# A four-layer graph network on one core: 28 destination blocks in seven full panels and 21 gathered, instead of 29 in eight panels and 20 gathered

## The chip, the core and the metric

The kernel runs on one core of a Trainium2 chip. The metric is the device time of one execution in microseconds (us). The engines are called as in the profile: PE is TensorE's matmul, PEld its weight load, DVE is VectorE, ACT is ScalarE, POOL is GpSimd and SP is SyncE. SP and POOL also issue the DMAs that matter here.

## What is computed

There are 6250 nodes with 256 features and 100,000 edges, sorted by destination. Each node's features are normalised and go through a relu. Then come four layers: each node adds up the features of its in-neighbours to its own, and a three-step MLP follows. The last layer's output is added to the input.

```python
def agg(h):
    return jax.ops.segment_sum(h[src], dst, num_segments=N)
for l in range(NL - 1):
    h = x + agg(x)
    h = jax.nn.relu(h @ W1s[l] + b1s[l])
    h = jax.nn.relu(h @ W2s[l] + b2s[l])
    x = h @ W3s[l] + b3s[l]
h = x + agg(x)
h = jax.nn.relu(h @ cW1 + cb1)
h = jax.nn.relu(h @ cW2 + cb2)
return h @ cW3 + cb3
...
h = jnp.maximum(_layernorm(x, axis=-1), 0.0)
x = x + _L0_gnn_ref(h, src, dst, ...)
```

## The kernel before

The 6250 nodes are cut into 49 blocks of 128 (the last has 106). The first matrix of a layer's MLP is applied before the sum over neighbours, since the two commute; W3 of one layer and W1 of the next are multiplied together once in the preparation. So a layer begins with a table of 49 blocks x 256 features, which lies in the chip's DRAM (`tables[l]`) and, split into a high and a low part, in SBUF (`XY`).

**Two ways to sum over neighbours.** For some destination blocks the edges are made into a dense matrix of counts, and the sum is a product with it: this is a *panel*. A panel is three or four destination blocks wide (384 or 512 columns). `product` runs over the 49 source blocks j; each j, called a *unit*, takes four matmuls (two halves of 128 features, high and low part) of the panel's width (L1334). The counts are bytes in DRAM (`mats`). `fetch` loads them in chunks of seven source blocks (L1033), and `prepare` turns each block into float on ACT or DVE (L1310, L1312) a few units ahead.

The other destination blocks are *gathered*. Each block's edges are held in 18 tiles of 128. For every tile POOL issues an indirect DMA that fetches the 128 source rows (L1198), and PE adds them up by products with a one-hot matrix that DVE makes (L1223, L1242: 44 small matmuls for a block). `finish` adds the block's own row, turns it over on PE, and after every four blocks calls `mlp`. All this is done by the class `Gathered`, one object for a layer.

**Which block goes where.** `gone` lists the gathered blocks as (first block, number), and `panels` the others. The last panel, blocks 44 to 47, is also the last but one entry of `gone`: in the first layer it is gathered, and afterwards it is a panel.

```python
gone = [(0, 4), (4, 4), (8, 4), (12, 4), (16, 3), (44, 4), (48, 1)]
panels = [(19, 3), (22, 4), (26, 4), (30, 4), (34, 3), (37, 3), (40, 4), (44, 4)]
```

The first layer thus has 7 panels (25 blocks) and 24 gathered blocks, the later ones 8 panels (29 blocks) and 20 gathered.

**The first layer builds the matrices.** The byte matrices are made beside the first layer, by `build`: 16 steps for each block of a panel, in each two matmuls of one-hots (L1010) and a copy of their result to bytes, three of four on ACT (L1017) and the fourth on DVE (L1019). `PRE` units of two steps each stand ahead of the first panel, as many as its matrices need and four more.

**The order of the work.** The whole instruction order is written out by hand. `now` counts units, `later(n, f)` puts work n units on, and `tick` runs what is due. `when` gives each unit a length in advance: the panel's width in blocks plus 2 (in the first layer a share for the building comes on top; a unit of `PRE` counts 7). A block's gathered work is cut into two *visits*, of 12 and of 6 tiles. A layer's first visit is put `LEAD` after its beginning in that measure, the last one `TAIL` units before the end of its last panel, and the others evenly between them by their number of tiles (`begin`, `advance`). POOL's gathers are issued two visits ahead in the first layer and three in the others (`ahead`, `send`), into 24 row buffers in the first layer and 26 in the others.

**The change of layer.** A gather reads rows from anywhere in the table, so the first gather of a layer has to wait until the last block of its table is stored. `mlp` puts the products of a group of blocks into fixed units, one group behind the other (`free`). When `store` has written the 49th block it calls the next layer's `begin`, and with it the first gathers are issued. PE in the meantime begins the next layer's first panel, with the source blocks that are already back in `XY` (`reload`, `bring`, `split`). The block 48, the last of `gone`, and the last panel are the last two groups of a layer.

Of the kernel before, what the change touches and what calls it, by code (L numbers as in the profile page):

```python
# [396 lines left out]
def sorted_edges(  # L397
# [65 lines left out]

    gone = [(0, 4), (4, 4), (8, 4), (12, 4), (16, 3), (44, 4), (48, 1)]
    panels = [(19, 3), (22, 4), (26, 4), (30, 4), (34, 3), (37, 3), (40, 4), (44, 4)]
    S0 = 2 * panels[0][0]
    assert gone[-2] == panels[-1] and sorted(
        b + i for b, n in gone[:-2] + gone[-1:] + panels for i in range(n)) == list(range(NT))  # L470
# [430 lines left out]
    with tc.manual_schedule():  # L901
# [57 lines left out]
        def pair(hots, k):  # L959

            if k < len(batches):
                s = batches[k][1]
                pairs[s] = hots.tile([P, 2, GSUB, 2], BF16, name="pairs", bufs=3)
                nc.scalar.copy(pairs[s], clT[:, :, :, s - S0, None].to_broadcast([P, 2, GSUB, 2]))
# [9 lines left out]
        def low_hot(hots, k):  # L974
            if k < len(batches):
                p, s, q0 = batches[k]
                lo = hots.tile([P, BATCH, P], BF16, name="lo", bufs=2)
                one_hot(lo, lanes, pairs[s][:, 1, q0:q0 + BATCH, :], P)
                hot[k] = [lo]

        def high_hot(hots, k):
            if k < len(batches):
                p, s, q0 = batches[k]
                hi = hots.tile([P, BATCH, HW], BF16, name="hi", bufs=2)
                one_hot(hi, cols, pairs[s][:, 0, q0:q0 + BATCH, :], HW)
                hot[k].append(hi)

        def build(hots, ats, ps_b):


            each = GSUB // BATCH
            pair(hots, 0)
            low_hot(hots, 0)
            high_hot(hots, 0)
            step = 0
            for k, (p, s, q0) in enumerate(batches):
                i, half = divmod(s - 2 * panels[p][0], 2)
                if half == 0 and q0 == 0:
                    at = ats.tile([P, NT, P], U8, name="at", bufs=2)
                lo, hi = hot.pop(k)  # L1000
                if q0 == 0:
                    pair(hots, k + each)
                for q in range(0, BATCH, 2):
                    if q == 0:
                        low_hot(hots, k + 1)
                    elif q == 2:
                        high_hot(hots, k + 1)
                    bp = ps_b.tile([P, W], F32, name="bp")
                    for m in range(2):
                        nc.tensor.matmul(bp[:, m * HW:(m + 1) * HW], lo[:, q + m, :],  # L1010
                                         hi[:, q + m, :], start=True, stop=True)
                    d = half * 64 + (q0 + q) * GD
                    o = at[:, :, d:d + 2 * GD].rearrange("p h (i d) -> p h i d", i=2)
                    v = bp[:, :2 * HW].rearrange("p (i h d) -> p h i d", i=2, d=GD)
                    step += 1
                    if step % 4:
                        nc.scalar.copy(o, v)  # L1017
                    else:
                        nc.vector.tensor_copy(o, v)  # L1019
                    if half and q0 + q + 2 == GSUB:  # L1020
                        own = at[:, panels[p][0] + i, :]
                        nc.vector.tensor_tensor(own, own, ident, OP.add)
                        nc.sync.dma_start(out=mats[p][:, i, :], in_=at.rearrange("p h d -> p (h d)"))
                    yield
# [133 lines left out]
        class Gathered:  # L1158
            def __init__(self, l):
                self.l, self.sent, self.done = l, 0, 0  # L1160
                self.first = None
                self.end = ends[l] - TAIL
                self.blocks = [(b, n, i, left[q] + i * T)
                               for q, (b, n) in enumerate(gone) for i in range(n)
                               if l == 0 or (b, n) != panels[-1]]
                self.own = {}
                self.visits = [(g, rounds) for g in range(len(self.blocks)) for rounds in VISITS[l > 0]]
                self.n = len(self.visits)
                self.rows = {}

                self.upto = [0]
                for _, rounds in self.visits:
                    self.upto.append(self.upto[-1] + 2 * len(self.tiles(rounds)))
# [3 lines left out]
                return sorted({k for r in rounds for k in ROUNDS[r] if k is not None})  # L1177

            def begin(self, t):
                self.first = when[t] + LEAD  # L1180
                self.pace = (when[self.end] - self.first) / (self.upto[-1] - self.upto[1])

            def send(self, upto):
# [95 lines left out]
        PRE = (GSUB * panels[0][1] + EARLY) // 2  # L1279
# [1 line left out]
        units = [(0, -1, j) for j in range(PRE)] + [  # L1281
            (l, p, j) for l in range(NLAYER + 1) for p in range(last[l] + 1) for j in range(NT)]
        ahead = [2, 3]
        LEAD, TAIL = 75, 8

        ends = [PRE + NT * sum(k + 1 for k in last[:l + 1]) for l in range(NLAYER + 1)]
        when = [0.0]
# [76 lines left out]
        with tc.tile_pool(name="hots", bufs=1) as hots, tc.tile_pool(  # L1364
            name="ats", bufs=1
        ) as ats, tc.tile_pool(name="rings", bufs=AHEAD + 2) as rings, tc.tile_pool(
            name="gath", bufs=24
        ) as gath, tc.tile_pool(
            name="ps_a", bufs=2, space=PSUM
        ) as ps_a, tc.tile_pool(name="ps_b", bufs=2, space=PSUM) as ps_b:  # L1370
            layers[0].begin(0)
            layers[0].send(ahead[0])
            beside = build(hots, ats, ps_b)
            while now[0] < PRE:
                for _ in range(2):
                    next(beside)
                    built[0] += 1
                tick()
                layers[0].advance()
                if built[0] == GSUB * panels[0][1]:  # L1380
                    for _ in range(3):
                        fetch(0, 0)
            for p in range(last[0] + 1):
                product(0, p, ps_a, beside)
            assert next(beside, None) is None and built[0] == total
# [13 lines left out]
def kernel(  # L1399
# [26 lines left out]
    good = keep.tile([1, 1], I32, name="good")  # L1426
    rest = (x, src, dst, W1s, b1s, W2s, b2s, W3s, b3s, cW1, cb1, cW2, cb2, cW3, cb3, out)
    sorted_edges(tc, good, *rest)
    done = nc.values_load(good[0:1, 0:1], min_val=0, max_val=1)
    with tc.If(done == 0):  # L1430
# [27 lines left out]
```

## Time and profile before

| | |
|---|---|
| median of 3 runs | 2232.75 us (2231.62 to 2237.27) |
| the profiled execution | 2230.63 us, its span 2228.8 us |
| granted TensorE clock, mean | 0.983 |
| panel matmuls L1334 | 6076 (3724 of 512 columns, 2352 of 384) |
| gathers L1198 | 1512, first at 144.7 us, last at 2200.4 us, median 953 ns |
| matmuls of gathered rows L1242 | 3696, 281.5 us busy |
| transposes L1264 | 168, 31.9 us busy |
| build matmuls L1010 | 928, 136.0 us busy |
| casts L1310 on ACT, L1312 on DVE | 943 and 576 |

The span is the time from the first to the last instruction of the profiled execution. The preparation lasts until about 145 us, the first layer until about 731 us, and the others end near 1230, 1727 and 2215 us. The time between two layers cannot be read from PE's busy share, since PE already works on the next layer's first panel while the last blocks of the old one are finished.

### The profile page before, as it was taken

The numbers are of one execution on the slowest core, as the hardware profiler recorded it, in microseconds if no ns is written. First come the engines' busy times: TensorE is split into PE (matmuls) and PEld (weight loads), VectorE is DVE, ScalarE is ACT, GpSimd is POOL, SyncE is SP. The second block draws the span as 40 slices with busy tenths as digits, with TensorE's granted clock in tenths as the row PEclk, the third lists the DMA queues.
The fourth block names the chain that finished last, engine by engine and source line by source line (L and its number), as shares of the span: only waits on it lengthen the run. The fifth ranks groups of instructions, "written<-read, shape, count | busy, mean of one in ns | idle before, by whom it ended". The sixth has DMA issues, their size and how long they took to land.

```text
span 2228.8 us, 35398 instructions
## 1 busy us (share of the span) xinstructions
PE 2118.0 (95%) x12356; PEld 1559.5 (70%) x12356; DVE 918.2 (41%) x2723; ACT 920.1 (41%) x1915; POOL 1521.5 (68%) x1570
## 2 busy tenths in 40 slices
PE   4778999999999999999999999999999999999998
PEld 2555766667776777778877777778877766677765
DVE  6667465445656522223323422223323423333332
ACT  3666565666667422223334322322324423222222
POOL 2337777777776477777774577777774577777773
PEclk9888999999999999999999999999999999999999
DMA  5436575565666655555655655555655655666663
GB/s 173 134 120 201 185 227 173 178 211 174 200 205 225 195 168 172 165 156 170 193 167 172 191 173 169 157 161 180 187 163 166 204 173 177 184 184 186 191 186 102
DMA packets 264100, 395.56 MB, mean 177 GB/s; under 512 B 36353, under 2 KB 210028, under 8 KB 263912
## 3 DMA queue, kind: packets, MB, share of 16 engines
q0 software_dynamic: 73920, 200.88, 30.2%
q1 hardware_dynamic: 187936, 189.68, 26.8%
q10 hardware_dynamic: 2056, 2.65, 0.4%
q8 instruction: 99, 1.62, 0.3%
q14 instruction: 89, 0.73, 0.1%
HBM read 335.81 MB, written 57.26 MB: 176 GB/s over the span
## 4 chain that ended last, share of the span: by engine, by line
PE 65%; DMA 4%; issue 2%; POOL 1%; ACT 0%; DVE 0%; SPq 0%; POOLq 0%; DVEq 0%
PE agg L1334 45%; PE sums L1242 8%; PE ps L1099 5%; PE ps L1122 4%; DMA rows<-table,idx 3%; POOL rows L1198 1%; PE ps L1119 1%; PE pt L1264 1%; PE bp L1010 1%; DMA xt<-in_x_dram 0%; ACT h L1347 0%; DMA own<-table 0%; DVE z L1127 0%; ACT at L1017 0%; ACT h L1268 0%
## 5 line engine op out<-in xcount | busy, mean ns | idle before, releaser
L1198 POOL DMA_INDIRECT rows<-table,idx x1512 | 1484.3, 982 | 614.0 <-issue 243.5
L1334 PE MATMUL agg<-a,XY 128*128 128x512 f32 (+1 forms) x6076 | 1454.7, 386 | 3.6 <-ACT a L1310 3.2
L1334 PEld LDWEIGHTS agg<-a,XY 128*128 128x128 f32 x6076 | 1085.4, 189 | 239.1 <-issue 81.0
L1310 ACT CAST a<-at 128x512 fp32r<-128x512 uint8 (+1 forms) x943 | 537.0, 579 | 650.3 <-PE agg L1334 585.2
L1312 DVE CAST a<-at 128x512 fp32r<-128x512 uint8 (+1 forms) x576 | 279.6, 490 | 498.7 <-PE agg L1334 455.0
L1242 PE MATMUL sums<-rows,hot 128*32 128x256 f32 x3696 | 281.5, 387 | 31.9 <-DMA rows<-table,idx 30.4
L1242 PEld LDWEIGHTS sums<-rows,hot 128*32 128x32 f32 x3696 | 119.4, 110 | 169.7 <-issue 54.7
L1017 ACT CAST at<-bp 128x392 uint8<-128x392 f32 x348 | 161.1, 490 | 142.8 <-PE bp L1010 139.9
L1099 PE MATMUL ps<-h,w 128*128 128x512 f32 (+5 forms) x392 | 164.3, 541 | 1.2 <-ACT h L1347 1.2
L1254 DVE TENSOR_TENSOR u<-sums,own 128x256 f32<-128x256 f32 x84 | 35.5, 423 | 291.7 <-PE sums L1242 291.7
L1010 PE MATMUL bp<-hi,lo 128*128 128x196 bf16 x928 | 136.0, 259 | 19.9 <-DVE hi L969 11.7
L1223 DVE TENSOR_TENSOR hot<-colf,rel 128x64 f32<-128x64 f32 x924 | 140.6, 217 | 12.3 <-PE sums L1242 11.9
L1122 PE MATMUL ps<-w,h 128*128 128x256 f32 x588 | 140.0, 379 | 0.0
L1010 PEld LDWEIGHTS <-lo 128*128 128x128 bf16 x928 | 71.9, 100 | 94.8 <-issue 43.9
L969 DVE TENSOR_TENSOR lo<-lanes,pairs 128x512 bf16<-128x512 bf16 x232 | 97.1, 419 | 84.0 <-PE bp L1010 58.4
L969 DVE TENSOR_TENSOR hi<-cols,pairs 128x784 bf16<-128x784 bf16 x232 | 129.6, 559 | 0.0
L1122 PEld LDWEIGHTS ps<-w,h 128*128 128x128 f32 x588 | 111.0, 189 | 15.7
L1268 ACT ACTIVATE h<-pt,bias 128x256 f32<-128x256 f32 (+1 forms) x92 | 36.9, 453 | 199.1 <-PE pt L1264 199.1
L1101 ACT ACTIVATE h<-ps,bias 128x512 f32<-128x512 f32 (+5 forms) x98 | 62.4, 637 | 109.6 <-PE ps L1099 109.6
L1131 DVE TENSOR_TENSOR zz<-ps,w 128x512 f32<-128x512 f32 (+1 forms) x81 | 51.7, 638 | 130.9 <-PE ps L1122 130.9
L1099 PEld LDWEIGHTS ps<-h,w 128*128 128x128 f32 (+1 forms) x392 | 68.2, 181 | 51.3 <-issue 29.4
L1019 DVE CAST at<-bp 128x392 uint8<-128x392 f32 x116 | 65.5, 565 | 91.9 <-PE bp L1010 90.3
(134 smaller groups left out, 716.6 us busy)
## 6 DMA issues: line engine op xcount, KB each, us to landing
at<-mat SPq DMA_DIRECT2D x133, 448.0 KB
at<-mat SPq DMA_DIRECT2D x84, 336.0 KB
rows<-table,idx POOLq DMA_INDIRECT x1512
mat<-at SPq DMA_DIRECT2D x29, 784.0 KB
table<-zz SPq DMA_DIRECT2D x66, 256.0 KB
back<-table SPq DMA_DIRECT2D x126, 128.0 KB
own<-table SPq DMA_DIRECT2D x80, 128.0 KB
xs<-in_x_dram SPq DMA_DIRECT2D x8, 768.0 KB
```

The costliest lines, as they stand in the source:

```text
L969: nc.vector.tensor_tensor(o.rearrange("p q (n t) -> p q n t", t=2), values.rearrange("p (n t) -> p n t", t=2)[:, None, :, :].to_broadcast( ...
L1010: nc.tensor.matmul(bp[:, m * HW:(m + 1) * HW], lo[:, q + m, :], hi[:, q + m, :], start=True, stop=True)
L1017: nc.scalar.copy(o, v)
L1019: nc.vector.tensor_copy(o, v)
L1099: nc.tensor.matmul(ps[:mp, :w], weights[l][0][:, c, i * P:i * P + mp], h1[:, c, :w], start=(c == 0), stop=(c == KC - 1))
L1122: nc.tensor.matmul(o, h2[0][:, c, nodes], w3[:, c, :], start=(c == 0), stop=(c == KC - 1))
L1198: nc.gpsimd.indirect_dma_start(out=t, out_offset=None, in_=tables[self.l][:, :], in_offset=bass.IndirectOffsetOnAxis(ap=idx[:, o:o + 1], a ...
L1223: nc.vector.tensor_tensor(hot[:, i, :, :], colf[:, None, i * Q:(i + 1) * Q].to_broadcast([P, 2, Q]), rel[:, o + k:o + k + TS + 1:TS, None] ...
L1242: nc.tensor.matmul(self.sums[(2 * h + m) * Q:(2 * h + m + 1) * Q, :C], self.hots[r, m][:, h, :], self.rows[g, h, k], start=(r == 0), stop= ...
L1310: nc.scalar.copy(o, mat[l, p][j])
L1312: nc.vector.tensor_copy(o, mat[l, p][j])
L1334: nc.tensor.matmul(agg[c][:, :w], XY[:, j, o:o + P], a[:, :w], start=(j == 0 and half == 0), stop=(j == NT - 1 and half == 1))
```

## The change

Block 19 goes from the panels to the gathered blocks. The remaining 28 blocks form seven panels of four, where there were eight panels of three or four. The first layer, which leaves the last panel out, has six panels (24 blocks) and 25 gathered blocks, the later ones seven panels and 21 gathered blocks.

```diff
-    gone = [(0, 4), (4, 4), (8, 4), (12, 4), (16, 3), (44, 4), (48, 1)]
-    panels = [(19, 3), (22, 4), (26, 4), (30, 4), (34, 3), (37, 3), (40, 4), (44, 4)]
+    gone = [(b, 4) for b in range(0, 20, 4)] + [(44, 4), (48, 1)]
+    panels = [(b, 4) for b in range(20, 48, 4)]
```

In the build, the copies of the steps ahead of the first panel all go to ACT. `PRE` grows from 28 units to 36 by itself, because the first panel now has four blocks.

```diff
                     step += 1
-                    if step % 4:
+                    if step % 4 or step <= 2 * PRE:
                         nc.scalar.copy(o, v)
```

The first and last visit of a layer are placed anew in the later layers; the first layer keeps 75 and 8.

```diff
-                self.end = ends[l] - TAIL
+                self.end = ends[l] - (TAIL if l else 8)
...
-                self.first = when[t] + LEAD
+                self.first = when[t] + (LEAD if self.l else 75)
...
-        LEAD, TAIL = 75, 8
+        LEAD, TAIL = 90, 2
```

## The prediction

> **What bounds the kernel now.** I read the page first. Its busy shares point at TensorE (PE), and the row of GpSimd (POOL) in the 40 slices has a shape worth following: 7 in nearly every slice, with a dip at each change of layer.
>
> ```profile
> PE 2118.0 (95%) x12356; PEld 1559.5 (70%) x12356; DVE 918.2 (41%) x2723; ACT 920.1 (41%) x1915; POOL 1521.5 (68%) x1570
> ...
> POOL 2337777777776477777774577777774577777773
> ```
>
> So I asked next what POOL's gathers (L1198) wait for. The columns are the total in us, the number of waits, and the longest of them.
>
> ```profile
> POOL rows L1198 <- issue: 243.5, 799, 0.3
> POOL rows L1198 <- DMA own<-table: 112.9, 3, 40.9
> POOL rows L1198 <- PE agg L1334: 90.8, 298, 0.3
> POOL rows L1198 <- PE sums L1242: 50.6, 166, 0.3
> POOL rows L1198 <- DVE lo L969: 41.5, 1, 41.5
> ```
>
> Of 1512 gathers only four wait longer than 0.3 us: the first one, and the first of each later layer. All others follow the one before after the same 0.3 us, whoever is named as the releaser; the name is then an accident. A queue that was held by a buffer or by PE would show waits of many lengths. The gathers stand back to back. The third view gives the busy time of L1198 alone, by stretch between those four waits.
>
> ```profile
> 144.00:713.00 569.00, 436.76 (x432) 0.97 0.62 198
> 713.00:746.00 33.00, 0.00 (x0) 1.00 0.40 120
> 746.00:1204.00 458.00, 347.89 (x360) 1.00 0.60 179
> 1204.00:1244.00 40.00, 0.00 (x0) 1.00 0.36 107
> 1244.00:1703.00 459.00, 349.09 (x360) 1.00 0.59 179
> 1703.00:1741.00 38.00, 0.00 (x0) 1.00 0.36 107
> 1741.00:2202.00 461.00, 350.60 (x360) 1.00 0.61 185
> ```
>
> The whole span is therefore 144.7 us before the first gather, four solid runs of gathers (1.317, 1.272, 1.275 and 1.281 us each), three gaps (33.4, 40.9 and 38.6), and 27 us behind the last gather. What happens in a gap is read from the timeline, here of the first.
>
> ```profile
> 711.89 0.95 POOL L1198 DMA_INDIRECT rows<-table,idx  x1 [0.30 <-issue]
> ...
> 719.11 1.50 PE L1242 MATMUL sums<-rows,hot 128*32 128x256 f32 x20
> ...
> 730.74 0.69 ACT L1347 ACTIVATE h<-agg,bias 128x512 f32<-128x512 f32 x1 [3.69 <-PE agg L1334]
> ...
> 746.21 0.95 POOL L1198 DMA_INDIRECT rows<-table,idx  x1 [33.38 <-DMA own<-table]
> ```
>
> The last visit's matmuls begin 6.3 us after the last gather has ended (14.1 and 11.6 in the two later gaps: PE is that far behind), and from there to the next layer's first gather it is 27.1, 26.8 and 27.0 us. PE is nearly full as well: it waits for rows only 31 times, 30.4 us in all. The two engines are close to balance, and POOL never pauses inside a layer.
>
> **What the change removes.** Per later layer, three panels of 384 columns and five of 512 become seven of 512; in the first, three and four become six. Either way that is 196 matmuls x (3 narrow - 2 wide). Their cadence is in the chain of waits:
>
> ```profile
> 1467.49 3.74 PE agg L1334 x16
> ...
> 1491.71 2.79 PE agg L1334 x16
> ```
>
> 0.234 us wide, 0.174 narrow, so 196 x (0.522 - 0.468) = 10.6 us a layer, 42 in all. The build loses 32 of 928 bp matmuls (136.0 us): 4.7. ACT and DVE lose 196 of 1519 casts, SP 28 of 217 chunk loads; none of the three is the path.
>
> **What it adds.** One more gathered block per layer: 18 gathers on POOL, 44 sums matmuls (281.5/84 = 3.4 us) and two transposes (31.9/84 = 0.4) on PE, and small work on DVE and ACT that their shares of 41% cover. For PE that is 3.7 us a layer, so PE wins 42 + 4.7 - 15 = 32 us net, and POOL gets 72 gathers more.
>
> The preparation treats 450 gather columns for 432; the list is ready at 111 us, and the first gather waits until 144.7 for the first table, so 34 us cover that.
>
> In the first layer 16 more build steps stand ahead of the first panel. 56 steps took 43 us (144.7 to 187.75); 72 at that rate take 55, fewer if the copies moved to ACT relieve DVE. Those 12 us are no cost while POOL, already gathering from 144.7, ends later than PE; without that cover (PE's last visit is at 719 now, POOL's run would end at 737) they would be paid whole. The wider leads and tails scale with the unit (4 matmuls of 0.234 for 4 of 0.174): 90/6 and 75/5 are both 15 units. They move when PE takes rows up, not when POOL asks for them.
>
> **Does POOL have room for them?** By the waits, no. Its next gather is always ready, so 18 more take 18 x 1.27 to 1.32 us, unless PE falls behind by the 24 to 26 row buffers, which it gets further from. Set against each other, PE's lateness of 14.1 us at the second gap would become 14.1 - 7 (PE's gain) + 5.6 (the visit put six units later) - 22.9 (POOL's addition) = -10 us: PE will wait for rows, and POOL's run sets the end. The 0.30 us behind every gather, also behind the first ones after a pause of 40 us, when nothing can be queued, says that it belongs to the gather.
>
> The Trainium skill speaks against this: "Trace Analysis", section "Identifying the Most-Contended Engine", takes occupancy as a fair measure of how near to its limit GpSimd is; by that rule the 76% of a layer (347.89 of 458) would leave a quarter of POOL free, and the time would be that of rival (1) below.
>
> **The gaps.** Check of the old one from the last visit on: sums 1.5, eight wide units 7.5, the one-block MLP 2.6, eight narrow units 5.6, the four-block MLP 7.6 (four groups of 1.88 and 1.89), last store to first gather 3.1 (1241.38 to 1244.45 in the second gap): 27.9 against 27. In the later layers the visit now stands two units before the end; the last panel's MLP queues behind block 48's, six units later. So 1.5 + 1.9 + 14 wide units 13.1 + 2.6 + 7.6 + 3.1 = 29.8, less the 0.9 that the check was over: 29. Landing of the last rows, not seen by itself, lies between 1.4 (in the last layer the matmuls begin 1.4 us after the last gather, unwaited) and 3.5 (PE's longest wait for rows); I take 2, nearer the row at the same place. Gap 31. The first layer keeps its tail of 8: 1.5 + 7.5 + 2.6 + 7.5 + 7.6 + 3.1 - 0.9 + 2 = 31 too. Three gaps: 93 for 112.9.
>
> **The end.** Now 27.2 us behind the last gather, 14.2 of them behind the last aggregation. Then: 2 + 1.6 + 1.9 + 14.2, and block 48's two small products ahead of the last panel's on PE (0.65, a relu 0.4 with its signal 0.35, 0.7): 21.8.
>
> **The sum.** 144.7 + 450 x 1.317 (592.7) + 31 + 378 x 1.272 (480.9) + 31 + 378 x 1.275 (482.0) + 31 + 378 x 1.281 (484.1) + 21.8 = 2299 us span, for 2228.8 now. The profiled run took 2230.63, 1.8 more than its span, and the median of the runs is 2.1 above that: **2302 us**, 3.1% slower.
>
> **Rivals.** (1) POOL has room after all, because the 0.3 us are hidden waits on PE; then PE's sum decides: 2232.75 - 32 = 2201. For it: PE at 95%, and 65% of the chain of waits on PE. Against it: no wait of any length between 0.3 and 33 us. (2) PE stays late at the ends of the layers, as it does now by 11 us on average, since waiting for single rows all through the layer costs it its gain; three gaps of 40 in place of 31: 2329. For it: the margin is only 10 us a layer; against it: PE's work shrinks and POOL's grows. (3) The gaps and the tail give all back: 72 gathers cost about 91 us, and gaps and tail hold 140 us in all, so two thirds of that would have to go, although each gap has 27 us of chained work; a time around 2233.
>
> **How the numbers follow.** Forecast 0.79, rival (1) 0.05, (2) 0.12, (3) 0.04. Less than 0.3% (7 us) cannot be told from no change here. Rival (1) gives faster 0.05, (3) no change 0.03 with the rest slower: slower 0.92. The low end: the cadence of the undisturbed gather, 0.953 + 0.30 = 1.257, in half of the excess (1584 gathers, mean 1.288: -25), and gaps 2 us shorter: 2270. The high end is rival (2): 2328.
>
> **What would show it.** 1584 gathers with no wait over 0.3 us but four; runs of about 593 and 481 to 484 us; gaps near 31; wide agg cadence still 0.234; PE's waits for rows up from 30 to some 100 us, spread over the layers. Runs of gathers shorter than 470 us, or waits of POOL inside a layer on PE sums, would prove me wrong.

## The result, and the profile after

The changed kernel takes 2311.69 us (median of 4 runs, 2306.47 to 2313.69) where the kernel before takes 2233.82: a ratio of 1.0344, 95% interval 1.0321 to 1.0366. The forecast was 2302. The profiled execution took 2306.47 us, its span 2304.5.

First the page of the changed kernel: busy time by engine, POOL's row of the 40 slices, and the rows of the panel matmuls and of the gathered ones.

```profile
PE 2138.5 (93%) x11696; PEld 1453.6 (63%) x11696; DVE 856.8 (37%) x2648; ACT 885.9 (38%) x1778; POOL 1598.4 (69%) x1642
...
POOL 2337777777776477777775577777775677777774
...
L1334 PE MATMUL agg<-a,XY 128*128 128x512 f32 x5292 | 1404.0, 411 | 2.7 <-ACT a L1310 2.2
...
L1242 PE MATMUL sums<-rows,hot 128*32 128x256 f32 x3872 | 345.5, 391 | 88.1 <-DMA rows<-table,idx 86.6
```

The row of the gathered matmuls in the kernel before:

```profile
L1242 PE MATMUL sums<-rows,hot 128*32 128x256 f32 x3696 | 281.5, 387 | 31.9 <-DMA rows<-table,idx 30.4
```

PE runs 660 instructions fewer and is still "busier", by 20 us. The gathered matmuls show how: four more blocks should have added 13 us, and they added 64. A visit's matmuls overlap when all rows are there; now they come one by one as rows land, and each counts alone. PE's busy time hides that it waits. Its waits for rows (us in total, times, longest) have gone from the first line to the second:

```profile
PE sums L1242 <- DMA rows<-table,idx: 30.4, 31, 3.5
PE sums L1242 <- DMA rows<-table,idx: 86.6, 96, 3.9
```

The gathers' waits on POOL (us in total, times, longest):

```profile
POOL rows L1198 <- issue: 263.6, 865, 0.3
POOL rows L1198 <- PE agg L1334: 109.5, 256, 30.9
POOL rows L1198 <- PE sums L1242: 67.7, 222, 0.3
POOL rows L1198 <- DMA own<-table: 62.7, 2, 32.1
POOL rows L1198 <- DVE lo L969: 41.3, 1, 41.3
```

The picture is that of before: the first gather, three changes of layer (one of them now put down to PE's agg), and 0.3 us everywhere else; a single wait of 1.2 us inside a layer is the exception. By stretch, L1198 alone:

```profile
144.00:740.00 596.00, 458.76 (x450) 0.96 0.61 191
740.00:772.00 32.00, 0.03 (x1) 1.00 0.41 128
772.00:1254.00 482.00, 366.52 (x378) 1.00 0.59 176
1254.00:1284.00 30.00, 0.00 (x0) 1.00 0.47 135
1284.00:1768.00 484.00, 367.63 (x378) 0.99 0.57 173
1768.00:1798.00 30.00, 0.00 (x0) 1.00 0.45 133
1798.00:2282.00 484.00, 368.27 (x378) 0.99 0.58 176
```

The gap after the second layer, in order of time:

```profile
1252.48 0.95 POOL L1198 DMA_INDIRECT rows<-table,idx  x1 [0.30 <-issue]
...
1256.87 1.50 PE L1242 MATMUL sums<-rows,hot 128*32 128x256 f32 x20
...
1261.71 0.70 ACT L1347 ACTIVATE h<-agg,bias 128x512 f32<-128x512 f32 x1
...
1284.34 1.16 POOL L1198 DMA_INDIRECT rows<-table,idx  x1 [30.90 <-PE agg L1334]
```

The same gap in the kernel before:

```profile
1202.48 1.03 POOL L1198 DMA_INDIRECT rows<-table,idx  x1 [0.30 <-issue]
...
1217.61 1.50 PE L1242 MATMUL sums<-rows,hot 128*32 128x256 f32 x20
...
1244.45 0.95 POOL L1198 DMA_INDIRECT rows<-table,idx  x1 [40.94 <-DMA own<-table]
```

The last visit follows the last gather's end (1253.4) by 3.4 us, where PE used to be 14.1 late, and the next gathers begin 27.5 us after it. So the account closes, from one profiled span to the other: the four runs of gathers 1943.9 to 2043.6 us, +99.7; the three gaps 112.9 to 93.6, -19.4; the end 27.3 to 23.1, -4.2; the start -0.4. Together +75.7, as much as the spans differ.

For the experiments it must be known that in the three groups of several kernels all runs were some 27% longer, the kernel before included (2836 to 2841 us), with waits of POOL for PE of up to 21 us inside the layers in the kept traces, so of these groups only ratios to the kernel before in the same group are given, and they are weak evidence.

### The profile page after: what moved, and what is told of

The parts are those of the page before. It is cut to its first block, busy times and chain, and to the rows that moved or that the text cites. A ratio compares the mean times of both kernels' runs of the same rounds, so it can differ in the third digit from the quotient of the medians.

```text
span 2304.5 us, 33758 instructions
## 1 busy us (share of the span) xinstructions
PE 2138.5 (93%) x11696; PEld 1453.6 (63%) x11696; DVE 856.8 (37%) x2648; ACT 885.9 (38%) x1778; POOL 1598.4 (69%) x1642
## 4 chain that ended last, share of the span: by engine, by line
PE 51%; DMA 11%; issue 4%; POOL 3%; DVE 0%; SPq 0%; ACT 0%; POOLq 0%; DVEq 0%
PE agg L1334 34%; DMA rows<-table,idx 11%; PE sums L1242 7%; PE ps L1099 5%; PE ps L1122 4%; POOL rows L1198 3%; PE ps L1119 1%; PE pt L1264 1%; PE bp L1010 0%; DMA xt<-in_x_dram 0%; DMA own<-table 0%; DVE xt L1112 0%; DVE z L1127 0%; SPq L506 0%; DVE h L1344 0%
## 5 line engine op out<-in xcount | busy, mean ns | idle before, releaser
L1198 POOL DMA_INDIRECT rows<-table,idx x1584 | 1561.2, 986 | 617.3 <-issue 263.6
L1334 PE MATMUL agg<-a,XY 128*128 128x512 f32 x5292 | 1404.0, 411 | 2.7 <-ACT a L1310 2.2
L1334 PEld LDWEIGHTS agg<-a,XY 128*128 128x128 f32 x5292 | 968.8, 190 | 294.3 <-issue 84.7
L1310 ACT CAST a<-at 128x512 fp32r<-128x512 uint8 x819 | 502.6, 622 | 711.4 <-PE agg L1334 650.1
L1242 PE MATMUL sums<-rows,hot 128*32 128x256 f32 x3872 | 345.5, 391 | 88.1 <-DMA rows<-table,idx 86.6
L1312 DVE CAST a<-at 128x512 fp32r<-128x512 uint8 x504 | 228.1, 458 | 534.6 <-PE agg L1334 488.3
L1242 PEld LDWEIGHTS sums<-rows,hot 128*32 128x32 f32 x3872 | 132.5, 110 | 283.4 <-DMA rows<-table,idx 162.1
L1099 PE MATMUL ps<-h,w 128*128 128x512 f32 (+2 forms) x364 | 163.1, 570 | 0.3 <-ACT h L1347 0.3
L1010 PEld LDWEIGHTS <-lo 128*128 128x128 bf16 x896 | 71.5, 100 | 96.5 <-issue 42.8
L1101 ACT ACTIVATE h<-ps,bias 128x512 f32<-128x512 f32 (+2 forms) x91 | 60.6, 667 | 114.2 <-PE ps L1099 114.2
L1019 DVE CAST at<-bp 128x392 uint8<-128x392 f32 x94 | 53.1, 565 | 100.3 <-PE bp L1010 99.3
```

The lines of the kernel that those rows point to most:

```text
L1099: nc.tensor.matmul(ps[:mp, :w], weights[l][0][:, c, i * P:i * P + mp], h1[:, c, :w], start=(c == 0), stop=(c == KC - 1))
L1101: later(2, lambda: nc.scalar.activation(h2[0][:mp, i, :w], ps[:mp, :w], AF.Relu, bias=b2[l][:mp, i:i + 1]))
L1198: nc.gpsimd.indirect_dma_start(out=t, out_offset=None, in_=tables[self.l][:, :], in_offset=bass.IndirectOffsetOnAxis(ap=idx[:, o:o + 1], a ...
L1242: nc.tensor.matmul(self.sums[(2 * h + m) * Q:(2 * h + m + 1) * Q, :C], self.hots[r, m][:, h, :], self.rows[g, h, k], start=(r == 0), stop= ...
L1310: nc.scalar.copy(o, mat[l, p][j])
L1312: nc.vector.tensor_copy(o, mat[l, p][j])
```

## Experiments

### The gathers alone

The kernel before, with 18 more gathers in each layer that nothing reads. In the first form they stand behind the first 18 visits, in the second behind every second visit. Panels, lead, tail and the build's copies stay as before.

```diff
+                    if self.sent % 2 == 0 and self.sent < 2 * T:
+                        t = spare.tile([P, C], F32, name="unread")
+                        o = self.blocks[g][3]
+                        nc.gpsimd.indirect_dma_start(
+                            out=t, out_offset=None, in_=tables[self.l][:, :],
+                            in_offset=bass.IndirectOffsetOnAxis(ap=idx[:, o:o + 1], axis=0),
+                        )
                     self.sent += 1
...
+        spare = ctx.enter_context(tc.tile_pool(name="spare", bufs=2))
...
-        gath = ctx.enter_context(tc.tile_pool(name="gath2", bufs=26))
+        gath = ctx.enter_context(tc.tile_pool(name="gath2", bufs=25))
```

(The first form has `if self.sent < T:`.)

> The kernel before, with 18 more gathers in each layer into a spare tile that nothing reads (one behind each of the first 18 visits) and one row buffer less; no work on PE, ACT or DVE is added. Theory: each run of gathers grows by 23 us, 92 in all, of which PE's lateness at the gaps (6, 14 and 12 us) hides up to 30: 2234 + 92 - 30 = 2296, between 2280 and 2325. Rival (POOL has room, the 0.3 us behind a gather is a hidden wait): no change, 2234 within 10.

Measured in the group: a ratio of 1.0411 (1.0370 to 1.0453). The forecast, divided by 2234, is 1.028 (1.021 to 1.041), so this stands at its upper edge.

> The same kernel as gathers_alone (before, with 18 unread gathers a layer more), run again for the same reason. Where the kernel before takes its 2234: theory 2296, between 2280 and 2325; rival (POOL has room) 2234 within 10.

Measured, again in a group: 1.0375 (1.0292 to 1.0459), inside the range.

> The kernel before with 18 more gathers in each layer that nothing reads, one behind every second visit, and one row buffer less; nothing on PE, ACT or DVE. Theory: runs of about 593, 482, 483 and 485 us as after the change, gaps of 29 to 33: 2305, between 2285 and 2322. Rival (POOL has room): 2234 within 10. If only PE's new order costs: 2234 as well.

Measured in a group: 1.0277 (1.0193 to 1.0361); the forecast as a ratio is 1.032 (1.023 to 1.039).

> The kernel of gathers_alone_even alone in its group, since all groups of several kernels ran 27% long and the one single kernel didn't. Theory (POOL's run sets the layer): four runs of gathers of about 593, 482, 483 and 485 us with no wait inside them, gaps of 29 to 33, waits of PE for rows up from 30 us; 2305, between 2285 and 2322. Rival (POOL has room, or only PE's new order costs): 2234 within 10, with waits of POOL inside the layers.

Measured, alone: 2306.38 us against 2234.86, a ratio of 1.0319 (1.0299 to 1.0339). The forecast was 2305. POOL's busy time by stretch (all its instructions), and of PE's waits the one for rows (us in total, times, longest):

```profile
144.00:741.00 597.00, 459.76 (x450) 0.96 0.61 193
741.00:772.00 31.00, 0.11 (x1) 1.00 0.38 116
772.00:1254.00 482.00, 366.41 (x378) 1.00 0.59 177
1254.00:1284.00 30.00, 0.51 (x2) 1.00 0.43 127
1284.00:1766.00 482.00, 365.97 (x378) 0.99 0.59 176
1766.00:1795.00 29.00, 0.00 (x0) 1.00 0.41 120
1795.00:2276.00 481.00, 365.52 (x378) 0.99 0.60 182
```

```profile
PE sums L1249 <- DMA rows<-table,idx: 67.0, 71, 2.6
```

PE's waits for rows have more than doubled, from 30.4 us, and its busy time is 2155.9 us for 2118.0 with the same 12356 matmuls. The runs of gathers and the gaps are those of the changed kernel within 3 us each, although nothing reads the added rows and PE, ACT and DVE are given exactly the work that they had before. One gather inside a layer waits 1.4 us, all others 0.3, so the missing row buffer does not show either. That settles the cause: 72 more entries in POOL's queue cost 71.5 us by themselves, and the rest of the change (32 us less work on PE, the lead, the tail, the copies) is worth nothing that shows: 1.0344 and 1.0319 have intervals that overlap. The 0.3 us behind each gather are no room.

An added gather also moves 128 KB, so the run itself tells the queue from PE's order, but not POOL's issuing from the transfer. The DMA packets in the traces do. In the three gaps of the kernel before, POOL starts the layer's second gather 1.25 us after the first, while the first packet of the first gather moves only 1.9 to 2.4 us after that gather's start: POOL keeps its cadence before any row has moved. And the transfers keep up. Counted by the bytes of the queue, the median time from POOL's end to a gather's last packet is 1.5 to 1.9 us in every quarter of every run of gathers (in this kernel, the kernel before and the changed one), and not longer at the end of a run than at its start. Transfers that were the limit would fall further and further behind.

### The gathers taken away

The changed kernel without the gathers of block 19; its matmuls read the block's own rows in their place.

```diff
                         for h in range(2):
+                            if self.blocks[g][0] == 16 and self.blocks[g][2] == 3:
+                                self.rows[g, h, k] = self.own[g][:, 0, :]
+                                continue
                             t = gath.tile([P, C], F32, name="rows")
```

> The changed kernel, but block 19's 18 gathers in each layer are left out; its matmuls read the block's own rows instead, so PE's work and order stay. Theory (POOL's back-to-back gathers set the time): 1512 gathers, runs of about 569, 458, 459 and 461 us as before the change, PE late again by some 8 us at each of the three gaps: 2312 - 92 + 25 = 2245, between 2215 and 2260. Rival (PE's order, the places of the first and last visits, or the panels' shape cost the time): nothing of that is changed, so 2300 or more.

Measured in the group: 1.0117 (1.0058 to 1.0176). The forecast as a ratio is 1.005 (0.991 to 1.012).

> The same kernel as no_gathers_19 (block 19's 18 gathers a layer left out, PE's work and order as after the change), run again because the runs of that group were 27% longer with the kernel before too, PE standing still for stretches of up to 20 us that no instruction in the trace ends. Where the kernel before takes its 2234: theory (POOL's back-to-back gathers) 2245, between 2215 and 2260; rival (PE's order or the shape of the panels) 2300 or more.

Measured, again in a group: 1.0071 (1.0032 to 1.0109).

> The kernel of no_gathers_19 once more, to have it where the kernel before takes its 2234 us. Theory (POOL's back-to-back gathers): 2245, between 2215 and 2260, with four runs of gathers of about 569, 458, 459 and 461 us. Rival (PE's order or the shape of the panels): 2300 or more, with shorter runs and longer gaps.

Measured, alone: 2280.86 us (2 runs) against 2236.94, a ratio of 1.0205 (1.0157 to 1.0254). This misses the forecast by 36 us, and lies outside its range. The runs of gathers did shrink, to 581, 460, 459 and 462 us, but the later gaps grew to 48.6 and 47.1 and the end to 42.7. The second gap of this kernel shows why:

```profile
1215.44 1.50 PE L1245 MATMUL sums<-own,hot 128*32 128x256 f32 x20
...
1217.43 1.14 POOL L1201 DMA_INDIRECT rows<-table,idx  x1 [0.31 <-issue]
...
1227.23 1.50 PE L1245 MATMUL sums<-rows,hot 128*32 128x256 f32 x24
...
1239.77 1.50 PE L1245 MATMUL sums<-rows,hot 128*32 128x256 f32 x20
```

POOL's last gather ends at 1218.6. PE by then has just finished block 19's second visit (`sums<-own`, with no rows to wait for) and has block 48's two visits still ahead, pinned to units 12 us apart: 21.2 us from the last gather to the last visit, where it was 3.4. I had taken block 19's gathers out where they stood, near the end of each layer. Up to there PE is held up by POOL as in the changed kernel, and its order is fixed, so it cannot do the rest sooner. The place of a gather in the layer matters as well as the number: time saved on POOL behind the point up to which PE was held is not saved. This is read off this one trace; no undisturbed run tests it. The steps of that expectation that failed: PE was put 8 us late at each gap, and came 21.2 and 19.5 us after the last gather in the two later ones (3.9 in the first); the end was taken as unchanged, and PE came 20.9 us late there too; and the first run shrank to 581 us, not 569, with a wait of 5.6 us on PE inside it. From one profiled execution to the other, the end makes up 20 us of the miss, the runs 12 and the gaps 9. The rival's 2300 was not reached either: some 31 of the 75 us came back with the gathers.

So I took the same number out evenly, one of the 18 tiles of 18 blocks in each layer:

```diff
+                            if h and k == 3 and g < T:
+                                self.rows[g, h, k] = self.own[g][:, 0, :]
+                                continue
```

> The changed kernel with as many gathers as before the change, the 72 left out spread evenly: the first 18 blocks of each layer gather 17 tiles, and the matmuls of the 18th read the block's own rows. PE's work and order stay. It differs from no_gathers_19 in that no hole stands at the end of a layer. Theory (POOL's run sets the layer): runs of 569, 459, 460 and 462 us, gaps of 31 to 40: 2228, between 2210 and 2250. Rival (the new order on PE costs the most, and 31 us are all that 72 gathers are worth, as no_gathers_19_c gave): 2280, not under 2265.

Measured in a group: 0.9739 (0.9661 to 0.9817), that is 2.6% faster than the kernel before there, where the forecast as a ratio is 0.997 (0.989 to 1.007). The rival, 1.014 or more, would have the new order on PE cost something, and this ratio shows no such cost. But it was seen only in a group: there, a kernel with one block more in the panels (below) has the same ratio of 0.9739, and alone that kernel gains nothing. What the even removal takes alone is open, so that taking the gathers away gives their time back is not shown.

### The split of the blocks alone

```diff
-                    if step % 4 or step <= 2 * PRE:
+                    if step % 4:
...
-                self.end = ends[l] - (TAIL if l else 8)
+                self.end = ends[l] - TAIL
...
-                self.first = when[t] + (LEAD if self.l else 75)
+                self.first = when[t] + LEAD
...
-        LEAD, TAIL = 90, 2
+        LEAD, TAIL = 75, 8
```

> The changed split of the blocks alone: lead 75 and tail 8 in all layers and the build's copies as before. Theory: the gathers are as many, so the four runs are the same; the gaps stay near 31 us, the end is some 5 us longer with the tail of 8: 2317, between 2305 and 2330. Rival (the later last visit, which puts the last panel's MLP behind block 48's, costs the time): 20 us or more below the changed kernel, 2290 or less.

Measured in the group: 1.0247 (1.0187 to 1.0308). The loss is there without the new lead, tail and copies. But the forecast as a ratio is 1.037 (1.032 to 1.043), so the ratio misses it, and meets the bound of the rival, 1.025 or less. The changed kernel itself was not in that group, so what these three are worth beside it is not measured. The single runs bound it: against the unread gathers, which keep the old lead, tail and copies, the changed kernel's three gaps are 2.9 us longer together, its end is 4.0 shorter and its runs are 2.5 longer. No 20 us lie in the later last visit there.

### One block the other way

The kernel before with 30 blocks in 8 panels and 19 gathered:

```diff
-    gone = [(0, 4), (4, 4), (8, 4), (12, 4), (16, 3), (44, 4), (48, 1)]
-    panels = [(19, 3), (22, 4), (26, 4), (30, 4), (34, 3), (37, 3), (40, 4), (44, 4)]
+    gone = [(0, 4), (4, 4), (8, 4), (12, 4), (16, 2), (44, 4), (48, 1)]
+    panels = [(18, 4), (22, 4), (26, 4), (30, 4), (34, 3), (37, 3), (40, 4), (44, 4)]
```

> The kernel before, moved the other way: block 18 goes from the gathered ones to the first panel, which becomes (18, 4); 30 blocks in 8 panels, 19 gathered. 72 gathers fewer; PE gets 196 x (0.234 - 0.174) - 3.7 = 8 us a layer more and 5 us of building. Theory: POOL is no longer the bound, PE's waits for rows (84 us with its weight loads) mostly go: 2234 + 37 - 50 = 2221, between 2195 and 2250, and POOL waits inside a layer for PE. Rival (PE's work alone sets the time): 2234 + 37 = 2271.

Measured in the group: 0.9721 (0.9691 to 0.9751). The forecast as a ratio is 0.994 (0.983 to 1.007), so this misses it.

> The kernel of one_more_in_panels (block 18 from the gathered ones to the first panel; 30 blocks in 8 panels, 19 gathered) where the kernel before takes its 2234. Theory: POOL with 72 gathers less is no longer the bound; PE has 37 us more work and loses most of its 84 us of waits for rows: 2221, between 2195 and 2250, with waits of POOL on PE inside the layers. Rival (PE's work alone counts): 2271.

Measured, again in a group: 0.9739 (0.9661 to 0.9817), a miss too.

> The kernel of one_more_in_panels alone in its group. Theory: four runs of gathers of at least 545, 435, 436 and 438 us, stretched by waits of POOL for PE, which is now the bound: PE's 37 us more work less most of its 84 us of waits for rows give 2221, between 2195 and 2250. Rival (PE's work alone counts, as its 95% say): 2271.

Measured, alone: 2236.77 us against 2235.75, a ratio of 1.0005 (0.9996 to 1.0014): no change, where the groups gave a gain of 2.6 to 2.8%. L1198 by stretch, and its two waits with times over 0.3 us inside the layers:

```profile
144.00:712.00 568.00, 426.68 (x414) 0.96 0.61 193
712.00:756.00 44.00, 0.18 (x2) 1.00 0.45 139
756.00:1207.00 451.00, 331.81 (x342) 1.00 0.58 174
1207.00:1256.00 49.00, 0.36 (x1) 1.00 0.42 123
1256.00:1711.00 455.00, 330.69 (x342) 0.99 0.57 172
1711.00:1760.00 49.00, 0.44 (x1) 1.00 0.42 123
1760.00:2197.00 437.00, 332.95 (x342) 1.00 0.63 189
```

```profile
POOL rows L1198 <- PE sums L1242: 92.3, 146, 6.0
...
POOL rows L1198 <- PE bp L1010: 29.5, 92, 1.8
```

This is what POOL looks like when it is not the bound: waits of up to 6 us on the matmuls that free its buffers, 1.32 us for a gather in the second run where 1.27 is POOL's own pace, and gaps of 44 to 49 us, in which PE comes 16 to 21 us late. Only the last layer, whose MLP is lighter, still runs at 1.278. From one profiled span to the other, PE's busy time grew by 21 us and its idle time shrank by 14. I had expected 37 more and 50 less; the sum missed by 16 us though inside its range. The 50 was taken from PE's waits and its weight loads' waits added together, but those overlap: PE's own were 30.4 us, of which 16.1 stayed.

So with 20 gathered blocks the kernel stands where POOL and PE meet. One block less changes nothing, one more costs 3.4%. No version that beats the kernel before was found.

## Why the prediction was right

**POOL bounds each layer.** The step that decided was the reading of the waits: no gather waits inside a layer, so each one added counts in full. The runs of gathers came out at 595.6, 481.5, 483.4 and 483.2 us for 592.7, 480.9, 482.0 and 484.1. The unread gathers reproduce it without any change on PE. Rival (1), that the 0.3 us are hidden waits, falls with them, and with it the reading of POOL's 76% as a quarter of room: here the measurement goes against the rule that the prediction cites for it.

**The gaps.** 32.1, 30.9 and 30.6 us for 31 each. The parts were off both ways, so that the sums fit so well is in part luck: the last visits came 4.0, 3.4 and 3.0 us after the last gathers, not 2 (the bounds were 1.4 and 3.5), and the rest took 28.1, 27.5 and 27.6, not 29. Rival (2), that PE stays late as it did by 6 to 14 us, is refuted by the same 3 to 4 us.

**The end.** 23.1 us for 21.8. Block 48's small products do stand ahead of the last panel's, as reckoned.

**PE's saving.** The cadence of the wide matmuls is unchanged: in the last layer, the shortest sixteen take 3.75 us in the chain of waits before and 3.73 after. With the matmuls counted as forecast, the 42 us of work are saved, and PE waits for rows instead, 86.6 us for 30.4; the forecast said some 100.

**The first layer.** Its first panel began at 203.6 us, where 72 steps at the old rate gave 200: moving the copies to ACT did not speed the steps up. As the prediction said, this is covered by POOL's longer run and costs nothing.

**What was off.** The sum for the span was 2299 against 2304.5. The forecast took its runs from the edges of the windows (569 us for a run of 568.1), which made the four of them 3.3 us too long together. By the runs themselves a gather took 1.315, 1.270, 1.274 and 1.278 us before and 1.324, 1.274, 1.279 and 1.278 after: a slowing of 7 us in all that was not foreseen, half of it hidden by the edges. The step from the span to the median has a slip too, 2299 + 1.8 + 2.1 being 2303. The median stood 5.2 us above the profiled execution, not 2.1 as before. All this is within the range. The lead and the tail alone were never tried undisturbed, so that they cost nothing rests on the overlap of two intervals and on the gaps and ends of two traces.

## What to carry to other kernels

An engine can be at its limit at a busy share of 76%. The sign here was that each of its instructions followed the last after one and the same pause; count its instructions, multiply by the cadence, and compare that with the stage before moving work to it. Where two engines meet in a fixed order, work taken off one can turn into its waits for the other, and the busy time of the waiting engine can even rise. The proof, and a cheap test, is to add the suspected instruction alone, read by nothing, evenly over the stage.

## What the runs showed of the hardware

A gather of 128 rows of 1 KB takes POOL 0.953 us (median) and is followed by 0.30 us before the next one; POOL's row of the slices therefore stops at 7 tenths when it can do no more.

Its rows land behind it without holding it up: the last packet comes 1.5 to 1.9 us after POOL's end (medians by quarter of a run), early in a run and late.

PE's busy time counts the time once in which small matmuls overlap: 3696 of 387 ns each, in the mean, had 281.5 us in the kernel before. The same 3696 had 312.9 with the unread gathers, when more of them came one by one as rows landed.
